# A graph-attention kernel: gathered rows side by side in one ring, one reduction over the places

## The chip, the cores and the metric

The kernel runs on one core of a Trainium2 chip. The metric is the device time of one execution in microseconds; the kernel before took 2087.87 us (median of three runs, 2083.0 to 2097.82). Besides these runs there is one execution under the hardware profiler, whose instructions are what "the trace" and "the page" mean below.

The engines are called as in the profile: PE (matrix multiply; PEld is its weight load), DVE (vector), ACT (scalar functions and copies), POOL (here mostly the issue of indirect transfers, the gathers and scatters) and SP (issue of plain transfers).

## The reference

A graph of N = 3327 nodes with 256 features each and a 0/1 adjacency matrix (each node has itself and on average 8 others as neighbours) goes through four layers: attention block, averaging layer, attention block, attention block. An attention block has 8 heads of 32:

```python
qkv = layer_norm(x, g1, be1) @ w_qkv
q, k, v = (qkv[:, 0], qkv[:, 1], qkv[:, 2])          # after reshape(n, 3, 8, 32)
scores = jnp.einsum('nhd,mhd->hnm', q, k) * SCALE
scores = jnp.where((adj != 0)[None], scores, -jnp.inf)
attn = jax.nn.softmax(scores, axis=-1)
out = jnp.einsum('hnm,mhd->nhd', attn, v).reshape(n, DIM)
x = x + out @ w_proj + b_proj
x = x + jax.nn.gelu(layer_norm(x, g2, be2) @ w1 + b1) @ w2 + b2
```

The averaging layer weighs a 64-wide projection of the neighbours' rows, projects it back, adds it to x and normalises.

## The kernel before

The kernel makes use of the sparsity: no 3327 x 3327 score matrix exists. A first stage (`adjacency`, 0 to 310 us) reads the matrix, makes for every node the list of its neighbours (at most 24), and sorts the nodes by the number of neighbours. The sorted nodes are cut into 26 tiles of 128 (one node per partition); `ROOM[t]` says how many neighbour places tile t needs, from 24 for tile 0 down to 4 for tile 25, 228 together. Beside this, `by_node` computes keys, values and queries of the first block into a table in DRAM.

Then come block 0 (310 to 760 us), the averaging layer (760 to 1064), block 1 (to 1605) and block 2 (to the end). A block goes through the tiles from the one with the fewest places to tile 0 with 24, in ten groups (`GROUPS`) of two to four tiles, the last two of one. For each tile:

- `scores` (L552): the tile's own row is fetched (keys, values, queries, features, 4 x 256 floats; L559 by an indirect transfer in block 0, L564 and L566 by plain ones in blocks 1 and 2). In blocks 0 and 1 ACT copies its features to `x[t]` (L568). ACT copies the query into a PSUM bank (L571, two banks in rotation). For each place an indirect transfer (`gather`, L546) fetches key and value (512 floats) of one neighbour per partition. Four places make one unit tile; ten units are in rotation (`UNITS`), and three own rows. For the own row and for each unit DVE multiplies the keys by the query (L576) and sums over each head's 32 (L577). Then follow the mask, the maximum, the subtraction and, on ACT, the exponential (L591 to L596).
- `weighed` (L599), called for the tile before, after the scores of the next: sum and reciprocal of the exponentials, the scaled weights (L605 to L607), the multiplication of all values by the weights (L610: own row, then each unit), and the additions: full units onto the first one (L622), the part unit (L626), halves of the unit onto each other (L630, 512 and 256 elements), and the last onto the own part (L631).
- After a whole group: transposes and projection (`project`), residual (L671), layer norm, the two feed-forward products (L685 and L695), and what the next stage needs (`finish`, `write`). Each product's bias comes by a small matmul of three bf16 parts (`bias`, L189) that opens the accumulation of each tile's 256 columns; two tiles share one PSUM bank.

The statements are recorded by a tile framework, which orders the instructions of each engine by its own planning and adds the waits: a gather into a unit waits until DVE has done with the unit's earlier content. Each engine works through its own order; what waits at the head holds what is behind it. The averaging layer borrows the same units for transposed parts of the adjacency matrix (L936) and for rows (L955).

Of the kernel before, what the change touches and what calls it, by code (L numbers as in the profile page):

```python
# [59 lines left out]
UNIT = 4  # L60
UNITS = 10
# [20 lines left out]
def chunk_width(c):  # L82
    return min(CW, NP - c * CW)


class Sparse:
# [100 lines left out]
    def bias(self, y, i):  # L187

        self.nc.tensor.matmul(y, self.ones3, self.biases[:, i, :], start=True, stop=False)  # L189
# [354 lines left out]

    def gather(self, out, table, t, j, held):
        g = self.nc.gpsimd.indirect_dma_start(  # L546
            out=out, out_offset=None, in_=table,
            in_offset=bass.IndirectOffsetOnAxis(ap=self.ids[:, t, j : j + 1], axis=0),
        )
        self.after(g, held)  # L550

    def scores(self, pool, pp, layer, t, held):  # L552


        nc = self.nc
        J = ROOM[t]
        own = pool.tile([P, 4 * DIM], F32, tag="own", name="own", bufs=3)
        if layer == 0:
# [14 lines left out]
        units = []  # L573

        def dot(at, k, n):
            nc.vector.tensor_mul(k, k, query.unsqueeze(1).to_broadcast([P, n, DIM]))  # L576
            nc.vector.tensor_reduce(  # L577
                s[:, ds(at, n), :].rearrange("p j h -> p (j h)"), k.rearrange("p j (h d) -> p j h d", d=HD), AX.X,
                ALU.add,
            )  # L580
# [10 lines left out]
        nc.vector.tensor_add(s[:, ds(1, J), :], s[:, ds(1, J), :], away)  # L591
        top = pool.tile([P, HEADS], F32, tag="top", name="top", bufs=3)
        nc.vector.tensor_reduce(top, s[:, : J + 1, :].rearrange("p j h -> p h j"), AX.X, ALU.max)
        wide = [P, J + 1, HEADS]
        nc.vector.tensor_sub(s[:, : J + 1, :], s[:, : J + 1, :], top.unsqueeze(1).to_broadcast(wide))
        nc.scalar.activation(s[:, : J + 1, :], s[:, : J + 1, :], AF.Exp)  # L596
        return own, s, units

    def weighed(self, pool, t, own, s, units):  # L599

        nc = self.nc
        J = ROOM[t]
        wide = [P, J + 1, HEADS]
        total = pool.tile([P, HEADS], F32, tag="total", name="total", bufs=3)
        nc.vector.tensor_reduce(total, s[:, : J + 1, :].rearrange("p j h -> p h j"), AX.X, ALU.add)  # L605
        nc.vector.reciprocal(total, total)
        nc.vector.tensor_mul(s[:, : J + 1, :], s[:, : J + 1, :], total.unsqueeze(1).to_broadcast(wide))  # L607

        def weigh(to, v, at, n):
            nc.vector.tensor_mul(  # L610
                to.rearrange("p j (h d) -> p j h d", d=HD), v.rearrange("p j (h d) -> p j h d", d=HD),
                s[:, ds(at, n), :].unsqueeze(3).to_broadcast([P, n, HEADS, HD]),
            )

        o = pool.tile([P, DIM], F32, tag="o", name="o", bufs=5)
        weigh(o.unsqueeze(1), own[:, DIM : 2 * DIM].unsqueeze(1), 0, 1)
        for u, j0, n in units:
            v = u[:, :n, DIM:]
            weigh(v, v, 1 + j0, n)
        full = [u for u, _, n in units if n == UNIT]  # L620
        for u in full[1:]:
            nc.vector.tensor_add(full[0][:, :, DIM:], full[0][:, :, DIM:], u[:, :, DIM:])  # L622
        u = full[0]
        for r, _, n in units:
            if n < UNIT:
                nc.vector.tensor_add(u[:, :n, DIM:], u[:, :n, DIM:], r[:, :n, DIM:])  # L626
        n = UNIT
        while n > 1:
            n //= 2
            nc.vector.tensor_add(u[:, :n, DIM:], u[:, :n, DIM:], u[:, ds(n, n), DIM:])  # L630
        nc.vector.tensor_add(o, o, u[:, 0, DIM:])  # L631
        return o

    def block(self, layer, weights, then, ahead=None, last=None):
# [4 lines left out]
        with tc.tile_pool(name="bs", bufs=1) as pool, tc.tile_pool(name="bp", bufs=1, space=PSUM) as pp:  # L639
            begin, finish, write = then(pool, pp) if then else (None, None, None)  # L640
            held = self.held

            def attended(t, own, s, units):
                o = self.weighed(pool, t, own, s, units)
                return t, o

            def halves(name, n):

                banks = [pp.tile([P, CW], F32, tag="mm", name=name, bufs=4) for _ in range(0, n, 2)]
                return [banks[q // 2][:, ds(q % 2 * DIM, DIM)] for q in range(n)]  # L650

            def project(group, outs):
# [8 lines left out]
                for q, y in enumerate(ys):  # L661
                    self.bias(y, 2 * layer)
                    for k in range(KC):
                        nc.tensor.matmul(y, oT[:, k, ts(q, P)], wpj[:, k, :], start=False, stop=k == KC - 1)  # L664
# [11 lines left out]
            def feed_forward(group, ys):  # L676
# [15 lines left out]
                for q, y in enumerate(ys):  # L692
                    self.bias(y, 2 * layer + 1)
# [887 lines left out]
```

## Time and profile before

| what | value |
|---|---|
| median of three runs | 2087.87 us (2083.0 to 2097.82) |
| the profiled execution | 2096.42 us, span of its instructions 2094.6 us |
| mean granted PE clock in it | 0.77 |
| instructions | 17222 |
| gathers (L546) | 684, 975 ns of POOL each |
| transfers | 369.73 MB, 169409 packets |
| features copied by ACT (L568) | 52 of 404 ns (median) |
| bias matmuls (L189) | 78 of 283 ns and 78 of 295 ns |

A line of the groups reads: source line, engine, operation, tile written <- tiles read, shapes (partitions x elements of a partition), count | busy time in us, mean ns of one | idle time of the engine just before these instructions, and what ended that idle time. A line of windows gives for a stretch of the span the busy time of each engine with its number of instructions.

### The profile page before, as it was taken

The numbers are of one execution on the slowest core, as the hardware profiler recorded it, in microseconds if no ns is written. First come the engines' busy times: TensorE is split into PE (matmuls) and PEld (weight loads), VectorE is DVE, ScalarE is ACT, GpSimd is POOL, SyncE is SP. The second block draws the span as 40 slices with busy tenths as digits, with TensorE's granted clock in tenths as the row PEclk, the third lists the DMA queues.
The fourth block names the chain that finished last, engine by engine and source line by source line (L and its number), as shares of the span: only waits on it lengthen the run. The fifth ranks groups of instructions, "written<-read, shape, count | busy, mean of one in ns | idle before, by whom it ended". The sixth has DMA issues, their size and how long they took to land. (4 is left out here: it accounts for less than half of the span.)

```text
span 2094.6 us, 17222 instructions
## 1 busy us (share of the span) xinstructions
PE 1263.4 (60%) x4806; PEld 812.1 (39%) x4806; DVE 1342.0 (64%) x3407; ACT 684.9 (33%) x1420; POOL 1001.0 (48%) x946
## 2 busy tenths in 40 slices
PE   3244411556755579699934688567695277655676
PEld 1122200344424337577512454343473154323445
DVE  3567635577776785165636789776732679976871
ACT  3555501233321224122322444334343133322232
POOL 3768757555555531101156645555203666565521
PEclk8667655677767769799976888798798587767778
DMA  8878827555555550858486656656215665565520
GB/s 191 330 300 326 284 79 213 160 163 154 170 148 175 147 131 23 198 154 230 160 284 205 216 166 209 220 178 193 61 56 201 210 186 176 176 190 160 152 65 20
DMA packets 169409, 369.73 MB, mean 177 GB/s; under 512 B 78821, under 2 KB 90291, under 8 KB 165976
## 3 DMA queue, kind: packets, MB, share of 16 engines
q0 software_dynamic: 68624, 222.01, 35.4%
q1 hardware_dynamic: 85689, 112.44, 17.1%
q10 hardware_dynamic: 14990, 34.08, 5.0%
q8 instruction: 40, 0.66, 0.1%
q14 instruction: 66, 0.54, 0.1%
HBM read 279.77 MB, written 77.59 MB: 171 GB/s over the span
## 5 line engine op out<-in xcount | busy, mean ns | idle before, releaser
L546 POOL DMA_INDIRECT unit<-kv,ids x684 | 667.2, 975 | 434.7 <-issue 189.1
L685 PE MATMUL f<-hT,w 128*128 128x256 f32 (+3 forms) x960 | 342.1, 517 | 58.6 <-ACT gT L688 23.2
L256 PE MATMUL tr<-ident,xh 128*128 128x128 f32 x312 | 80.6, 384 | 442.7 <-ACT xh L251 395.6
L695 PE MATMUL f<-w,gT 128*128 128x256 f32 x1248 | 306.4, 399 | 17.9 <-ACT gT L688 14.3
L685 PEld LDWEIGHTS f<-hT,w 128*128 128x128 f32 x960 | 190.4, 219 | 202.6 <-issue 106.0
L695 PEld LDWEIGHTS f<-w,gT 128*128 128x128 f32 x1248 | 238.3, 197 | 68.7 <-ACT gT L688 18.3
L256 PEld LDWEIGHTS tr<-ident,xh 128*128 128x128 f32 x312 | 41.7, 179 | 483.3 <-ACT xh L251 414.8
L576 DVE TENSOR_TENSOR unit<-unit,qs 128x1024 f32<-128x1024 f32 (+3 forms) x198 | 211.7, 1069 | 26.4 <-DMA unit<-kv,ids 15.0
L577 DVE TENSOR_REDUCE qs<-unit 128x32 f32<-128x1024 f32 (+3 forms) x198 | 212.7, 1074 | 4.8 <-DVE qs L607 1.7
L610 DVE TENSOR_TENSOR unit<-unit,qs 128x1024 f32<-128x1024 f32 (+3 forms) x198 | 210.0, 1065 | 0.0
L315 POOL TENSOR_TENSOR m<-a,place 128x3328 f16<-128x3328 fp8e4 x26 | 159.4, 6132 | 78.7 <-ACT a L313 78.6
L688 ACT ACTIVATE gT<-f,b 128x256 f32<-128x256 f32 (+3 forms) x240 | 124.8, 536 | 212.5 <-PE f L685 106.6
L538 PE MATMUL kvps<-wqkv,hT 128*128 128x512 f32 x312 | 171.9, 677 | 29.5 <-ACT hT L262 22.5
L326 DVE MAX8 found<-m 128x8 f16<-128x416 f16 x208 | 111.5, 579 | 39.7 <-POOL m L315 33.1
L664 PE MATMUL proj<-wproj,oT 128*128 128x256 f32 x312 | 109.3, 489 | 42.7 <-ACT oT L659 22.8
L576 DVE TENSOR_TENSOR own<-own,qs 128x256 f32<-128x256 f32 x78 | 32.3, 415 | 141.5 <-ACT qs L571 124.2
L658 PE MATMUL otr<-ident,o 128*128 128x128 f32 x156 | 25.5, 289 | 142.4 <-DVE qs L577 87.4
L990 POOL DMA_INDIRECT sorted<-st,to x26 | 24.8, 955 | 178.7 <-ACT st L542 147.1
L538 PEld LDWEIGHTS kvps<-wqkv,hT 128*128 128x128 f32 x312 | 63.2, 213 | 86.7 <-issue 37.7
L313 ACT ACTIVATE a<-a 128x3328 fp8e4<-128x3328 int32 x26 | 77.3, 2973 | 51.6 <-DMA kv<-st 29.0
L251 ACT ACTIVATE xh<-x,shift,rstd 128x256 f32<-128x256 f32 x104 | 58.4, 594 | 104.5 <-DVE shift L218 80.9
L664 PEld LDWEIGHTS proj<-wproj,oT 128*128 128x128 f32 x312 | 66.9, 235 | 65.6 <-ACT oT L659 28.4
(193 smaller groups left out, 1881.4 us busy)
## 6 DMA issues: line engine op xcount, KB each, us to landing
a<-in_adj SPq DMA_DIRECT2D x25, 1663.5 KB
kv<-st ACTq DMA_DIRECT2D x52, 512.0 KB
own<-sorted SPq DMA_DIRECT2D x26, 512.0 KB
unit<-kv,ids POOLq DMA_INDIRECT x684
adj<-a SPq DMA_DIRECT2D x26, 416.0 KB
own<-qkv SPq DMA_DIRECT2D x26, 384.0 KB
own<-own SPq DMA_DIRECT2D x26, 384.0 KB
w<-in_L_gnn_w SPq DMA_DIRECT2D x6, 1024.0 KB
```

What stands on the lines that cost most here:

```text
L256: nc.tensor.transpose(ps[k][:, ts(q, P)], t[:, ts(k, P)], self.ident)
L315: nc.gpsimd.tensor_mul(m.rearrange("p (s e) -> p s e", e=SEG), a8.rearrange("p (s e) -> p s e", e=SEG), place.unsqueeze(1).to_broadcast([P ...
L326: nc.vector.max(found[:, i, s, :], m[:, ts(s, SEG)])
L538: nc.tensor.matmul(kv, hT[:, k, ts(q, P)], w[:, k, DIM : 3 * DIM], start=k == 0, stop=k == KC - 1)
L546: g = self.nc.gpsimd.indirect_dma_start(out=out, out_offset=None, in_=table, in_offset=bass.IndirectOffsetOnAxis(ap=self.ids[:, t, j : j + ...
L576: nc.vector.tensor_mul(k, k, query.unsqueeze(1).to_broadcast([P, n, DIM]))
L577: nc.vector.tensor_reduce(s[:, ds(at, n), :].rearrange("p j h -> p (j h)"), k.rearrange("p j (h d) -> p j h d", d=HD), AX.X, ALU.add,)
L610: nc.vector.tensor_mul(to.rearrange("p j (h d) -> p j h d", d=HD), v.rearrange("p j (h d) -> p j h d", d=HD), s[:, ds(at, n), :].unsqueeze ...
L664: nc.tensor.matmul(y, oT[:, k, ts(q, P)], wpj[:, k, :], start=False, stop=k == KC - 1)
L685: nc.tensor.matmul(y[:, :w], w1[:, k, ts(f, P)], hT[:, k, :w], start=k == 0, stop=k == KC - 1)
L688: nc.scalar.activation(gT[-1][:, f % 2, :w], y[:, :w], AF.Gelu_apprx_tanh, bias=b1[:, f : f + 1])
L695: nc.tensor.matmul(y, gT[f // 2][:, f % 2, ts(q, P)], w2[:, f, :], start=False, stop=f == FC - 1)
```

## The change

All rows of a tile, gathered ones and its own, now lie side by side in one tile `ring` of 46 places of 512 floats (`RING`), in the order of the places with the own row (two places long) at the end. `take` hands out the places in rotation and begins again at the start when the rest is too short. Scores are computed in pieces of up to 6 places and weighed in pieces of up to 9, the own row among them, in pieces of nearly equal size. The weighed values are summed by one `tensor_reduce` over the places, whose input steps by a whole place from element to element, in place of the additions. The features go to `x[t]` by a transfer: in block 0 from the ring, in block 1 straight from DRAM; ACT's copy is gone. The bias matmul covers both 256-column halves of a bank at once, and only the last matmul of a bank closes its accumulation. The averaging layer takes four places at a time from the ring instead of a unit.

```diff
-UNIT = 4
-UNITS = 10
+RING = 46
+PIECE = 6
+WEIGHED = 9
...
+class Halves(list):
+    def __init__(self, banks, n):
+        super().__init__(banks[q // 2][:, ds(q % 2 * DIM, DIM)] for q in range(n))
+        self.banks = banks
+    def bank(self, q):
+        return self.banks[q // 2], min(2, len(self) - q)
+    def ends(self, q):
+        return q % 2 == 1 or q == len(self) - 1
...
-    def bias(self, y, i):
-        self.nc.tensor.matmul(y, self.ones3, self.biases[:, i, :], start=True, stop=False)
+    def bias(self, ys, q, i):
+        if q % 2 == 0:
+            bank, n = ys.bank(q)
+            self.nc.tensor.matmul(
+                bank[:, : n * DIM], self.ones3, self.biases[:, i, :].unsqueeze(1).to_broadcast([3, n, DIM]),
+                start=True, stop=False,
+            )
...
+    def take(self, n):
+        if self.at + n > RING:
+            self.at = 0
+        at = self.at
+        self.at += n
+        return self.ring[:, at : at + n, :]
...
-        own = pool.tile([P, 4 * DIM], F32, tag="own", name="own", bufs=3)
+        n = J + 1
+        rows = self.take(n + 1)
+        own = rows[:, J:, :].rearrange("p a b -> p (a b)")
         if layer == 0:
             nc.gpsimd.indirect_dma_start(
                 out=own, out_offset=None, in_=self.kv[0][:],
                 in_offset=bass.IndirectOffsetOnAxis(ap=self.row[t], axis=0),
             )
+            nc.sync.dma_start(out=self.x[t], in_=own[:, 3 * DIM :])
         elif layer == 1:
-            self.after(nc.sync.dma_start(out=own, in_=self.sorted[ts(t, P), :]), self.turning)
+            for to, at in ((own[:, : 3 * DIM], self.sorted[ts(t, P), : 3 * DIM]), (self.x[t], self.sorted[ts(t, P), 3 * DIM :])):
+                self.after(nc.sync.dma_start(out=to, in_=at), self.turning)
         else:
             nc.sync.dma_start(out=own[:, : 3 * DIM], in_=self.own[t])
-        if layer < 2:
-            nc.scalar.copy(self.x[t], own[:, 3 * DIM :])
+        for j in range(J):
+            self.gather(rows[:, j, :], self.places[layer], t, j, held)
...
-        dot(0, own[:, :DIM].unsqueeze(1), 1)
-        for j0 in range(0, J, UNIT):
-            n = min(UNIT, J - j0)
-            u = self.units.tile([P, UNIT, 2 * DIM], F32, tag="unit", name="unit")
-            for j in range(n):
-                self.gather(u[:, j, :], self.places[layer], t, j0 + j, held)
-            dot(1 + j0, u[:, :n, :DIM], n)
-            units.append((u, j0, n))
+        for lo, w in self.pieces(n, PIECE):
+            k = rows[:, ds(lo, w), :DIM]
+            nc.vector.tensor_mul(k, k, query.unsqueeze(1).to_broadcast([P, w, DIM]))
+            nc.vector.tensor_reduce(
+                s[:, ds(lo, w), :].rearrange("p j h -> p (j h)"), k.rearrange("p j (h d) -> p j h d", d=HD), AX.X,
                 ALU.add,
             )
...
+    def pieces(n, most):
+        count = -(-n // most)
+        at = 0
+        for k in range(count):
+            w = (n - at) // (count - k)
+            yield at, w
+            at += w
...
+        for lo, w in self.pieces(n, WEIGHED):
+            v = rows[:, ds(lo, w), DIM:].rearrange("p j (h d) -> p j h d", d=HD)
+            nc.vector.tensor_mul(v, v, s[:, ds(lo, w), :].unsqueeze(3).to_broadcast([P, w, HEADS, HD]))
         o = pool.tile([P, DIM], F32, tag="o", name="o", bufs=5)
-        weigh(o.unsqueeze(1), own[:, DIM : 2 * DIM].unsqueeze(1), 0, 1)
-        for u, j0, n in units:
-            v = u[:, :n, DIM:]
-            weigh(v, v, 1 + j0, n)
-        full = [u for u, _, n in units if n == UNIT]
-        for u in full[1:]:
-            nc.vector.tensor_add(full[0][:, :, DIM:], full[0][:, :, DIM:], u[:, :, DIM:])
-        u = full[0]
-        for r, _, n in units:
-            if n < UNIT:
-                nc.vector.tensor_add(u[:, :n, DIM:], u[:, :n, DIM:], r[:, :n, DIM:])
-        n = UNIT
-        while n > 1:
-            n //= 2
-            nc.vector.tensor_add(u[:, :n, DIM:], u[:, :n, DIM:], u[:, ds(n, n), DIM:])
-        nc.vector.tensor_add(o, o, u[:, 0, DIM:])
+        nc.vector.tensor_reduce(o, rows[:, :n, DIM:].rearrange("p j f -> p f j"), AX.X, ALU.add)
         return o
...
-                    at = self.units.tile([P, NT // 2, HALF], BF, tag="unit", name="at")
+                    at = self.take(4).rearrange("p a b -> p (a b)").bitcast(BF)[:, : NT // 2 * HALF]
...
-                        both = self.units.tile([P, 2, 4 * DIM], F32, tag="unit", name="st4")
+                        both = self.take(4).rearrange("p (n a) b -> p n (a b)", n=2)
...
-        with tc.tile_pool(name="units", bufs=UNITS) as self.units:
+        with tc.tile_pool(name="gathered", bufs=1) as pool:
+            self.ring, self.at = pool.tile([P, RING, 2 * DIM], F32, name="ring"), 0
```

More of the change, by code (lines that the diff above doesn't have):

```diff
@@ L572, in scores @@
         s = bank[:, ds(DIM, (SLOTS + 1) * HEADS)].rearrange("p (j h) -> p j h", h=HEADS)
-        units = []
-        def dot(at, k, n):
-            nc.vector.tensor_mul(k, k, query.unsqueeze(1).to_broadcast([P, n, DIM]))
+        for lo, w in self.pieces(n, PIECE):
+            k = rows[:, ds(lo, w), :DIM]
+            nc.vector.tensor_mul(k, k, query.unsqueeze(1).to_broadcast([P, w, DIM]))
             nc.vector.tensor_reduce(
-                s[:, ds(at, n), :].rearrange("p j h -> p (j h)"), k.rearrange("p j (h d) -> p j h d", d=HD), AX.X,
+                s[:, ds(lo, w), :].rearrange("p j h -> p (j h)"), k.rearrange("p j (h d) -> p j h d", d=HD), AX.X,
@@ L579, in dot @@
                 ALU.add,
             )
[L582 to L589 removed]
         away = self.away[:, t, :J].unsqueeze(2).to_broadcast([P, J, HEADS])
[L591 removed]
+        nc.vector.tensor_add(s[:, :J, :], s[:, :J, :], away)
@@ L592, in scores @@
         top = pool.tile([P, HEADS], F32, tag="top", name="top", bufs=3)
[L593 to L599, printed above, removed]
+        nc.vector.tensor_reduce(top, s[:, :n, :].rearrange("p j h -> p h j"), AX.X, ALU.max)
@@ L601, in weighed @@
+        nc.vector.tensor_sub(s[:, :n, :], s[:, :n, :], top.unsqueeze(1).to_broadcast([P, n, HEADS]))
+        nc.scalar.activation(s[:, :n, :], s[:, :n, :], AF.Exp)
+        return rows, s
+    @staticmethod
+    def pieces(n, most):
[5 more added lines that the diff above has]
+            at += w
+    def weighed(self, pool, t, rows, s):
         nc = self.nc
-        J = ROOM[t]
-        wide = [P, J + 1, HEADS]
+        n = ROOM[t] + 1
@@ L604, in weighed @@
         total = pool.tile([P, HEADS], F32, tag="total", name="total", bufs=3)
-        nc.vector.tensor_reduce(total, s[:, : J + 1, :].rearrange("p j h -> p h j"), AX.X, ALU.add)
+        nc.vector.tensor_reduce(total, s[:, :n, :].rearrange("p j h -> p h j"), AX.X, ALU.add)
         nc.vector.reciprocal(total, total)
[L607 to L613, printed above, removed]
@@ L627, in weighed @@
-        n = UNIT
-        while n > 1:
-            n //= 2
-            nc.vector.tensor_add(u[:, :n, DIM:], u[:, :n, DIM:], u[:, ds(n, n), DIM:])
-        nc.vector.tensor_add(o, o, u[:, 0, DIM:])
+        nc.vector.tensor_mul(s[:, :n, :], s[:, :n, :], total.unsqueeze(1).to_broadcast([P, n, HEADS]))
+        for lo, w in self.pieces(n, WEIGHED):
+            v = rows[:, ds(lo, w), DIM:].rearrange("p j (h d) -> p j h d", d=HD)
+            nc.vector.tensor_mul(v, v, s[:, ds(lo, w), :].unsqueeze(3).to_broadcast([P, w, HEADS, HD]))
@@ L641, in block, with attended @@
             held = self.held
-            def attended(t, own, s, units):
-                o = self.weighed(pool, t, own, s, units)
-                return t, o
+            self.at = 0
+            def attended(t, rows, s):
+                return t, self.weighed(pool, t, rows, s)
             def halves(name, n):
-                banks = [pp.tile([P, CW], F32, tag="mm", name=name, bufs=4) for _ in range(0, n, 2)]
-                return [banks[q // 2][:, ds(q % 2 * DIM, DIM)] for q in range(n)]
+                return Halves([pp.tile([P, CW], F32, tag="mm", name=name, bufs=4) for _ in range(0, n, 2)], n)
             def project(group, outs):
@@ L661, in project @@
                 for q, y in enumerate(ys):
-                    self.bias(y, 2 * layer)
+                    self.bias(ys, q, 2 * layer)
                     for k in range(KC):
-                        nc.tensor.matmul(y, oT[:, k, ts(q, P)], wpj[:, k, :], start=False, stop=k == KC - 1)
+                        nc.tensor.matmul(
+                            y, oT[:, k, ts(q, P)], wpj[:, k, :], start=False, stop=k == KC - 1 and ys.ends(q)
+                        )
                 return ys
@@ L692, in feed_forward @@
                 for q, y in enumerate(ys):
-                    self.bias(y, 2 * layer + 1)
+                    self.bias(ys, q, 2 * layer + 1)
                     for f in range(FC):
                         nc.tensor.matmul(
-                            y, gT[f // 2][:, f % 2, ts(q, P)], w2[:, f, :], start=False, stop=f == FC - 1
+                            y, gT[f // 2][:, f % 2, ts(q, P)], w2[:, f, :], start=False, stop=f == FC - 1 and ys.ends(q)
                         )
@@ L935, in sums @@
                 for lo in range(0, n // 2):
-                    at = self.units.tile([P, NT // 2, HALF], BF, tag="unit", name="at")
+                    at = self.take(4).rearrange("p a b -> p (a b)").bitcast(BF)[:, : NT // 2 * HALF]
+                    at = at.rearrange("p (g i) -> p g i", i=HALF)
                     nc.sync.dma_start_transpose(
```

## The prediction

> **What bounds the kernel now.** I read the page's busy times first, then stage windows, then groups by form, and last the waits and the chain.
>
> ```profile
> PE 1263.4 (60%) x4806; PEld 812.1 (39%) x4806; DVE 1342.0 (64%) x3407; ACT 684.9 (33%) x1420; POOL 1001.0 (48%) x946
> ```
>
> No engine is full, so the stages decide. The windows below (start and end, length, busy of PE, PEld, DVE, ACT, POOL, granted clock, DMA share, GB/s) are the adjacency stage, block 0, the averaging, block 1 and block 2.
>
> ```profile
> 0.00:310.00 310.00, 107.00 (x303) 55.55 (x303) 169.63 (x583) 128.99 (x157) 202.65 (x131) 0.69 0.76 252
> 310.00:760.00 450.00, 235.86 (x810) 153.47 (x810) 316.77 (x698) 123.40 (x302) 259.22 (x267) 0.70 0.57 167
> 760.00:1064.00 304.00, 269.82 (x1441) 189.27 (x1442) 154.91 (x550) 92.48 (x208) 37.01 (x40) 0.91 0.56 155
> 1064.00:1605.00 541.00, 367.94 (x1257) 229.69 (x1256) 356.52 (x834) 207.76 (x472) 250.83 (x255) 0.81 0.55 176
> 1605.00:2095.00 490.00, 282.81 (x995) 184.11 (x995) 344.14 (x744) 132.24 (x282) 251.28 (x255) 0.75 0.50 152
> ```
>
> The change is in the blocks, 1481 us; DVE is the busiest engine in blocks 0 and 2, and in block 1 PE is level with it. Block 2 cut finer shows two regimes:
>
> ```profile
> 1605.00:1700.00 95.00, 30.69 (x97) 21.19 (x97) 55.14 (x135) 17.46 (x44) 58.83 (x61) 0.60 0.65 202
> 1700.00:1800.00 100.00, 58.03 (x209) 39.72 (x210) 89.37 (x204) 31.84 (x68) 62.09 (x63) 0.76 0.61 190
> 1800.00:1900.00 100.00, 69.32 (x195) 37.91 (x195) 74.89 (x155) 32.07 (x56) 57.38 (x60) 0.75 0.57 169
> 1900.00:2000.00 100.00, 59.01 (x213) 38.67 (x213) 76.76 (x143) 20.23 (x41) 60.78 (x61) 0.78 0.57 166
> ```
>
> In the chain that ended last, 1609 to 1731 us is almost all gathers, one per 1.25 us (0.95 and a gap of 0.30): POOL binds there and DVE is 58% busy at first. From 1734 on the chain is mostly DVE with stretches of PE and a few gathers, and POOL in turn waits for DVE to give back buffers:
>
> ```profile
> L546 POOL DMA_INDIRECT unit<-kv,ids x684 | 667.2, 975 | 434.7 <-issue 189.1 <-DVE o L631 64.4 <-DVE unit L622 54.7
> L576 DVE TENSOR_TENSOR own<-own,qs 128x256 f32<-128x256 f32 x78 | 32.3, 415 | 141.5 <-ACT qs L571 124.2 <-DMA own<-own 12.0 <-issue 5.4
> ```
>
> The second line is the other half of that loop: DVE waits 124 us for the query copy, and that copy (L571) waits 78 us for the last weighing of an earlier tile. So DVE's length per tile matters in the later tiles and much less in the first twelve.
>
> **The sum over places.** The groups of before, by form:
>
> ```profile
> L577 DVE TENSOR_REDUCE qs<-unit 128x32 f32<-128x1024 f32 x144 | 175.7, 1220 | 2.2 <-remote 1.6 <-DVE qs L607 0.5
> L622 DVE TENSOR_TENSOR unit<-unit 128x1024 f32<-128x1024 f32 x66 | 80.2, 1216 | 0.0
> L630 DVE TENSOR_TENSOR unit<-unit 128x256 f32<-128x256 f32 x78 | 32.5, 417 | 1.8 <-DVE qs L591 1.2 <-DVE qs L595 0.5
> ```
>
> 1216 ns for 1024 elements and 417 for 256 give 1.04 ns an element. In the timeline, back to back, a 1024-element operation follows its predecessor after 1.13 us, though it is listed with 1.21; so an instruction occupies DVE for elements x 1.04 ns + 0.065 us. The neighbour lists sum to J = 228 places a block, 254 with the own ones.
>
> Before, the additions (L622, L626, L630, L631) are 354 instructions over 3 x 228 x 256 = 175,104 elements: 182 + 23 = 205 us. After, 78 reductions run over 3 x 254 x 256 = 195,072 elements. Their inner step is one place, 512 floats, so each element is read 2 KB from the one before. The trace has one sizeable reduction that jumps in SBUF (L382 reads `p t l -> p l t`, a step of 25 floats) and one of nearly the same shape without jumps:
>
> ```profile
> L382 DVE TENSOR_REDUCE larger<-more 128x25 bf16<-128x650 f32 x1 | 1.3, 1317 | 0.0
> ...
> L442 DVE TENSOR_REDUCE count<-tops 128x26 f32<-128x624 f32 x1 | 0.8, 793 | 0.0
> ```
>
> Taking 0.15 us off each as the fixed part of a duration, that is 1.80 against 1.03 ns an element. L382 also writes bf16, but L377 turns 650 fp32 elements into bf16 in 823 ns, the ordinary rate, so I lay the difference on the jumps. Bounds for the new sum: 195,072 x 1.04 ns + 78 x 0.065 = 208 us from below (the row without jumps), 195,072 x 2.03 ns (L382 with no fixed part) + 5 = 401 us from above. I take 1.80, the row that jumps: 351 + 5 = 356 us. Change: +151 (+3 to +196).
>
> The Trainium skill speaks for the lower end: "VectorE: DVE Perf Modes", section "Mode 1× (REGULAR) — the baseline", says that this mode, the only one a reduction has, gives one result a cycle and takes weird strides too. By it the sum would be the 208 us; the trace's L382 contradicts it. "Advanced Engine Details and Errata", section "SBUF Cachelines", says the other thing, that accesses to ever new 16-byte lines pay a penalty, without a size.
>
> **Larger pieces.** Scores (L576, L577) and weighing (L610) keep their elements: 508 + 254 places a block. Their instructions fall from 552 + 276 to 324 + 117 in all, 387 x 0.065 = -25 us. The same skill page, section "The TRN2 errata", puts the measured fixed part of a DVE operation near 150 cycles; by that, the 663 instructions gone with the additions' would be worth some 104 us (estimate) and not 43. The timeline's 1.13 us starts show that most of a duration's fixed part overlaps the neighbour.
>
> DVE in all: +151 - 25 = **+126 us** (-22 to +171), 42 a block. A tile of J places changes by (J+1) x 0.195 - 0.28 us: +0.7 at J=4, +1.5 at J=8, +4.6 at J=24.
>
> **How much is on the path.** The first twelve tiles (J sums to 72) carry 84 x 0.195 - 12 x 0.28 = 13 us of the 42; POOL's gathers hide them, and it would be +13 a block without that cover. The other 14 tiles carry 29 us. There the release of a tile's places lets the gathers run, which let the scores run, so the added time goes round the loop; but DVE has some 40 us of idle in 1731 to 2000, part of it waits for PE (L671) that a later DVE finds already over. I count 4 us as swallowed and 25 as paid, three blocks: +75. Bounds: 0, and all 42 x 3 = 126.
>
> **The ring.** Ten units of 4 places and three own rows of 2 make 46 places, as does the ring. Held against each other tile by tile, the ring's wrap cuts the last tiles short: the own row (its query gates every score) of J=12 and J=24 tiles goes where the tile two before lay, and waits for that tile's whole sum; before, it waited for the weighing three tiles back. In the trace such an own load that came late cost DVE 12.0 us once (row L576 above). Three or four such tiles a block: 0 from below, 12 us a block from above, taken as 0, since the scheduler can put another tile's weighing in between. All places of a tile now come back at once, after the sum; before, 4-place units came back one by one (POOL's L622 waits). This is in the loop above.
>
> **Features by a transfer.** 52 ACT copies of 404 ns (L568) go, 21 us of ACT, which is 33% busy; their waits for the own row (86.5 and 36.8 us) pass to the query copy, which needs the same row. SP issues 52 more transfers at 0.32 us; in block 0 each waits on SP for its own gather, and nothing that is soon needed stands behind it (begin's weights are ahead; the averaging's first transposes, at 765 us, come after the last of them and need free places anyway). In block 1 all features load at the stage's start. Gathers that reuse an own row now also wait for that transfer. Worth 0 to -21; taken as 0, as ACT's copies lie beside DVE's work. Uncovered it would be the query 0.4 us earlier.
>
> **One bias matmul for two halves.** 156 of some 280 ns become 90 of twice the columns: at most -18 us of PE at 60%, at least 0 (twice the columns at twice the time, +6). Only the last groups' PE chain (2030 to 2080) has no cover: taken as 0.
>
> **Sum.** The profiled execution took 2096.4 us (span 2094.6), 8.5 above the median of 2087.9. 2096.4 + 75 = 2171, and in terms of the median **2163 us**, +3.6%.
>
> **Rivals.**
> - *The jump costs nothing* (faster). If DVE reads a 2 KB step at 1.04 ns, DVE loses 22 us; two thirds count (29 of 42): -15; the copies and the bias matmuls may give another -15: 2058. It decides at the price where DVE's sum is level: (205 + 25 - 5) / 195,072 = 1.15 ns an element, 2.95 us for ten places. For it: L908, a strided 26-element read, takes 178 ns, as its unstrided neighbours do (26 elements are few). Against it: L382.
> - *The jump costs, but the idle of DVE swallows it*: DVE idles 464 us in the blocks, so +126 fits. At most a quarter is paid: 2088 + 0 to 31, say 2100. Against: POOL's waits for DVE (o, unit) show that the idle is itself part of the loop.
> - *The ring binds on top*: the own row late by 12 us a block, and all 42 paid from the first tile: 2088 + 126 + 36 = 2250, its lower half from 2205.
>
> **Chances.** Forecast 0.54 (2115 to 2205), jump free 0.20 (2035 to 2075), swallowed 0.13 (2080 to 2120), ring 0.13 (2205 to 2260). A measurement of this kernel can tell about 1% from no change: faster means below 2067, slower above 2109. Faster 0.16 (most of the free jump), same 0.11 (its rest and half of swallowed), slower 0.73. The range 2060 to 2235 leaves out about 0.11 below and 0.05 above; the forecast's own is 2115 to 2205.
>
> **What would show it.** Right: a reduction `o<-ring` with 128x2560 elements at about 4.7 us (ten places) and some 356 us in all; DVE near 1465 busy; the blocks 20 to 30 us longer each, the averaging within 5 us; the first 120 us of block 2 still at one gather per 1.25 us; L622 to L631 and the L568 copies gone. Wrong: that reduction at 2.8 us (free jump); DVE up with spans unchanged (swallowed); long waits of the query copy for own loads, or of POOL for a transfer, in the J=12 to J=24 tiles (ring).

## The result, and the profile after

The changed kernel takes **2161.17 us** (median of four runs, 2149.99 to 2164.51) against 2092.51 us for the kernel before in the same comparison (four runs, 2083.0 to 2097.82): 1.0324 times as long, 95% interval 1.0266 to 1.0381. The forecast was 2163 us, slower. The total fits; the parts that make it up do not, and the experiments are about that.

The first line of the changed kernel's page, the busy times:

```profile
PE 1244.6 (58%) x4740; PEld 817.9 (38%) x4740; DVE 1453.1 (67%) x2744; ACT 671.3 (31%) x1370; POOL 977.0 (45%) x946
```

DVE has 111.1 us more to do (1342.0 before) with 663 instructions fewer; PE, ACT and POOL have a little less. (The expectations below call DVE, PE, ACT, POOL and SP VectorE, TensorE, ScalarE, GpSimd and SyncE.) The windows of the changed kernel are cut here by its own indirect transfers, which give sharp marks: the adjacency stage, block 0 up to its last scatter into `between`, the averaging up to block 1's first gather, block 1 up to block 2's first gather, and block 2. The columns are those of the windows before.

```profile
0.00:311.00 311.00, 106.71 (x303) 55.13 (x303) 172.26 (x590) 130.81 (x177) 200.05 (x129) 0.69 0.75 249
311.00:837.00 526.00, 296.16 (x1129) 205.13 (x1129) 399.37 (x604) 152.02 (x356) 264.72 (x280) 0.74 0.59 169
837.00:1088.00 251.00, 203.89 (x1101) 139.19 (x1101) 106.85 (x414) 57.66 (x110) 28.36 (x32) 0.87 0.55 159
1088.00:1663.00 575.00, 364.01 (x1234) 233.65 (x1234) 392.41 (x613) 197.07 (x445) 241.22 (x254) 0.78 0.53 167
1663.00:2160.00 497.00, 273.80 (x973) 184.79 (x973) 382.18 (x523) 133.72 (x282) 242.70 (x254) 0.74 0.49 143
```

Cut at the same marks, the trace of before has 847.5 us to the end of block 0, then 223.7, 537.8 and 485.6. (The stages given ahead of the result end block 0 at 760 us. Its scatters into `between` run on to 847.6 us, so block 0 was 88 us longer and the averaging 80 us shorter than was taken there.) So the 65 us between the two spans are made up as follows: block 0 ends 10.8 us *earlier*, the averaging is **27.5 us longer**, block 1 is 37.4 longer, block 2 11.0 longer. DVE's additional work is spread evenly over the blocks (35 to 38 us each); the time is not.

The groups of the changed kernel by form, the new sum and beside it a product over adjacent words:

```profile
L609 DVE TENSOR_TENSOR ring<-ring,qs 128x1280 f32<-128x1280 f32 x75 | 110.8, 1481 | 70.0 <-DMA ring<-kv,ids 63.2 <-ACT qs L605 3.5 <-issue 2.0
...
L644 DVE TENSOR_REDUCE o<-ring 128x256 f32<-128x2560 f32 x12 | 54.2, 4520 | 0.4 <-PE otr L670 0.4
...
L644 DVE TENSOR_REDUCE o<-ring 128x256 f32<-128x6400 f32 x3 | 33.3, 11101 | 0.1
...
L644 DVE TENSOR_REDUCE o<-ring 128x256 f32<-128x1280 f32 x6 | 13.9, 2312 | 0.0
```

From 1280 to 6400 elements the sum grows by 8.79 us, 1.72 ns an element; the product of the first line does 1280 elements in 1.48 us where the sum takes 2.31. All 78 sums take 343.5 us.

In the averaging the difference stands in one group. PE's groups of that stage, first of before, then of after:

```profile
L944 PE MATMUL ups<-at,parts 128*128 128x256 fp8e4 (+1 forms) x676 | 78.2, 275 | 0.0
```

```profile
L959 PE MATMUL ups<-ring,parts 128*128 128x256 fp8e4 (+1 forms) x676 | 86.3, 291 | 16.5 <-DMA ring<-adj 16.5
```

The sums over neighbours, which never waited, now wait 16.5 us for the transposed adjacency; and the same products take 8.1 us more, with a granted clock of the stage of 0.87 instead of 0.92. PE is busy for 204 of the 251 us, so both count.

### The profile page after: what moved, and what is told of

It is laid out like the page before. It is cut to its first block, busy times and chain, and to the rows that moved or that the text cites. A ratio compares the mean times of both kernels' runs of the same rounds, so it can differ in the third digit from the quotient of the medians.

```text
span 2159.7 us, 16455 instructions
## 1 busy us (share of the span) xinstructions
PE 1244.6 (58%) x4740; PEld 817.9 (38%) x4740; DVE 1453.1 (67%) x2744; ACT 671.3 (31%) x1370; POOL 977.0 (45%) x946
## 5 line engine op out<-in xcount | busy, mean ns | idle before, releaser
L575 POOL DMA_INDIRECT ring<-kv,ids x684 | 647.4, 947 | 454.4 <-issue 191.7
L644 DVE TENSOR_REDUCE o<-ring 128x256 f32<-128x1792 f32 (+9 forms) x78 | 343.5, 4404 | 1.3 <-issue 0.8
L709 PE MATMUL f<-w,gT 128*128 128x256 f32 x1248 | 297.8, 394 | 39.9 <-issue 33.9
L609 DVE TENSOR_TENSOR ring<-ring,qs 128x1280 f32<-128x1280 f32 (+3 forms) x162 | 226.6, 1403 | 92.7 <-DMA ring<-kv,ids 64.7
L709 PEld LDWEIGHTS f<-w,gT 128*128 128x128 f32 x1248 | 240.0, 196 | 93.2 <-issue 53.6
L610 DVE TENSOR_REDUCE qs<-ring 128x40 f32<-128x1280 f32 (+3 forms) x162 | 227.3, 1408 | 15.1 <-remote 6.6
L642 DVE TENSOR_TENSOR ring<-ring,qs 128x1280 f32<-128x1280 f32 (+4 forms) x117 | 219.2, 1883 | 2.5 <-DVE qs L615 1.2
L685 DVE SCALAR_TENSOR_TENSOR x<-f,x 128x256 f32<-128x256 f32 x78 | 30.5, 417 | 134.1 <-PE f L709 83.4
L1005 POOL DMA_INDIRECT sorted<-ring,to x26 | 25.0, 963 | 206.1 <-ACT ring L563 167.9
L676 PE MATMUL proj<-wproj,oT 128*128 128x256 f32 x312 | 95.4, 455 | 28.6 <-ACT oT L671 26.9
L670 PE MATMUL otr<-ident,o 128*128 128x128 f32 x156 | 26.8, 305 | 145.5 <-issue 103.9
L605 ACT COPY qs<-ring 128x256 f32<-128x256 f32 x78 | 29.2, 376 | 217.0 <-DVE ring L642 89.6
```

Source lines behind the costliest of these rows:

```text
L575: g = self.nc.gpsimd.indirect_dma_start(out=out, out_offset=None, in_=table, in_offset=bass.IndirectOffsetOnAxis(ap=self.ids[:, t, j : j + ...
L610: nc.vector.tensor_reduce(s[:, ds(lo, w), :].rearrange("p j h -> p (j h)"), k.rearrange("p j (h d) -> p j h d", d=HD), AX.X, ALU.add,)
L642: nc.vector.tensor_mul(v, v, s[:, ds(lo, w), :].unsqueeze(3).to_broadcast([P, w, HEADS, HD]))
L644: nc.vector.tensor_reduce(o, rows[:, :n, DIM:].rearrange("p j f -> p f j"), AX.X, ALU.add)
L709: nc.tensor.matmul(y, gT[f // 2][:, f % 2, ts(q, P)], w2[:, f, :], start=False, stop=f == FC - 1 and ys.ends(q))
```

## The experiments

All edited kernels load the adjacency in the averaging by plain transfers: the transposition is left out, the sums there are of other nodes, and everything else is as it was. A transposing load was not run in an edited kernel. So the study has its own two base kernels, `c0_before` and `e0_changed`. The runs went to several chips, and the kernel before takes a different time on them: 1908 us on one, some 2070 to 2090 us on the others ("quick" and "slow" below). Kernels are compared on one kind of chip only.

All profiled runs cut at the marks used above, in us:

| run | chip | to the end of block 0 | averaging | block 1 | block 2 | span |
|---|---|---|---|---|---|---|
| before | slow | 847.5 | 223.7 | 537.8 | 485.6 | 2094.6 |
| after | slow | 836.8 | 251.2 | 575.2 | 496.6 | 2159.7 |
| c0_before | quick | 788.6 | 225.6 | 476.3 | 420.6 | 1911.2 |
| e0_changed | quick | 757.1 | 228.4 | 499.7 | 439.1 | 1924.3 |
| e1_adjacent_b | quick | 747.6 | 228.4 | 482.8 | 407.0 | 1865.9 |
| e2_halves_b | quick | 764.2 | 228.0 | 459.1 | 411.0 | 1862.4 |
| f0_before | slow | 837.4 | 224.5 | 526.8 | 482.0 | 2070.7 |
| f1_changed | slow | 841.6 | 234.7 | 567.9 | 496.8 | 2141.0 |
| f2_apart | slow | 839.2 | 231.8 | 570.8 | 489.6 | 2131.4 |
| e4_copies_b | slow | 841.0 | 230.8 | 569.2 | 489.6 | 2130.6 |
| e0_again | slow | 833.7 | 228.9 | 563.3 | 487.5 | 2113.4 |
| e2_again | slow | 813.0 | 228.5 | 536.9 | 474.7 | 2053.1 |
| e5_pieces | slow | 842.4 | 228.9 | 538.8 | 507.1 | 2117.1 |
| e6_ring40 | slow | 865.2 | 246.9 | 565.4 | 513.4 | 2190.9 |

### The two base kernels: plain loads

```diff
-                    nc.sync.dma_start_transpose(
-                        out=at, in_=self.adj[ds(c * P + lo * HALF, HALF), :].bitcast(BF)
-                    )
+                    nc.sync.dma_start(
+                        out=at.rearrange("p g i -> p (g i)"),
+                        in_=self.adj[ds(c * P + lo * HALF, HALF), :].bitcast(BF).rearrange("(p n) f -> p (n f)", n=2),
+                    )
```

In the kernel before:

> The kernel before, whose 13 transposing loads of the adjacency in the averaging are plain loads of the same bytes: the transposition is left out, and the sums over neighbours are of other nodes. All further kernels of this study have this edit too, so that they are compared with this one and with the changed kernel so edited. If the blocks don't feel it, as both theories hold, block 0 and the blocks 1 and 2 stand within 1% of 847.6, 537.8 and 485.6 us, and only the averaging (223.6 us) can move.

In the changed kernel:

> The changed kernel with the plain loads of the adjacency and nothing else. Theory (a load of the adjacency into the one ring waits there for rows that nodes some chunks before still hold): the averaging stays 15 to 30 us longer than that of the kernel before with the same edit, and TensorE's sums over neighbours wait for the load again; the blocks are longer by the 37 us of the first comparison. Rival (the transposing loads themselves were slow in the changed kernel): the averaging falls to within 8 us of the kernel before so edited, and the whole distance of 69 us to about 45.

`c0_before`: 1910.52 us, 1.0001 of the kernel before on that chip (0.998 to 1.0022). The edit costs the kernel before nothing. The expected stage times were missed by 7 to 13%, all in the blocks: they were taken from a slow chip.

`e0_changed`: 1925.57 us, 1.0073 of the kernel before (1.005 to 1.0096). With plain loads the averaging is 228.4 us against 225.6: the excess of 27.5 us is gone, as the *rival* expected (on a slow chip too: 228.9 us in `e0_again`). The whole distance is 17.5 us and not about 45: on the quick chip the blocks differ by -31.5, +23.4 and +18.5 us.

### The sum over adjacent words

```diff
-        nc.vector.tensor_reduce(o, rows[:, :n, DIM:].rearrange("p j f -> p f j"), AX.X, ALU.add)
+        flat = rows.rearrange("p j f -> p (j f)")[:, : n * DIM]
+        nc.vector.tensor_reduce(o, flat.rearrange("p (f j) -> p f j", j=n), AX.X, ALU.add)
```

> The changed kernel with plain loads of the adjacency, whose sum over the places reads as many numbers, but adjacent ones (the first n x 256 of the tile's rows) instead of one word in every 2 KB; it no longer sums the values of the places, all else stands. Theory (the jump of 2 KB is what the sum costs, and VectorE's time counts in the blocks): the 78 sums take 195,072 x 1.043 ns + 78 x 0.15 us = 215 us instead of 343.5, and of these 128 us less the blocks give back between a third (the blocks grew by 38 us for 111 us more of VectorE) and six tenths (the forecast's 75 of 126): 44 to 77 us below the changed kernel with plain loads; the averaging stays. Rival, the sum lies in VectorE's idle time: 215 us as well, but less than 12 us are given back. Rival, the access is not what costs: the sums stay above 300 us.

Measured: 1869.8 us, **55.8 us less than `e0_changed`**; 0.9787 of the kernel before (0.9759 to 0.9815). The groups by form of this kernel, the same three sizes as above:

```profile
L645 DVE TENSOR_REDUCE o<-ring 128x256 f32<-128x2560 f32 x12 | 33.8, 2813 | 0.1
...
L645 DVE TENSOR_REDUCE o<-ring 128x256 f32<-128x6400 f32 x3 | 20.4, 6811 | 0.0
...
L645 DVE TENSOR_REDUCE o<-ring 128x256 f32<-128x1280 f32 x6 | 8.9, 1483 | 0.0
```

1.04 ns an element; 214.6 us in all, where 215 was expected. Number of elements, of sums and of results are the same, so the step of 2 KB is what costs, 0.68 ns an element. DVE's busy time falls by 125.8 us (1446.5 to 1320.7), and the kernel gets back 44% of that. Idle time swallows the larger part, but not all: the rival of the swallowed sum (less than 12 us) falls.

### The sum by halves in place

```diff
-        nc.vector.tensor_reduce(o, rows[:, :n, DIM:].rearrange("p j f -> p f j"), AX.X, ALU.add)
+        while n > 1:
+            h = n // 2
+            to = o.unsqueeze(1) if n == 2 else rows[:, :h, DIM:]
+            nc.vector.tensor_add(to, rows[:, :h, DIM:], rows[:, ds(n - h, h), DIM:])
+            n -= h
```

> The changed kernel with plain loads of the adjacency, whose sum over the places is made by additions by halves in place: the first h places plus the last h, until one is left; 282 additions over adjacent words instead of 78 sums with jumps. Theory: 175,104 numbers x 1.04 ns + 282 x 0.15 us = 224 us instead of 343.5, and the blocks give back a third to six tenths of these 119 us: 40 to 71 us below the changed kernel with plain loads. Rival, the number of instructions is what counts and not the jump: 204 instructions more cost 13 us at 0.065 us each, 0 to 14 us above it. Rival, the sum lies in idle time: within 10 us of it.

Measured on the quick chip: 1866.91 us, 58.7 below `e0_changed`, and **0.9769 of the kernel before** (0.9743 to 0.9794). Two lines of its groups, and between them how DVE's idle time moved; first `e0_changed`:

```profile
L644 DVE TENSOR_REDUCE o<-ring 128x256 f32<-128x1792 f32 (+9 forms) x78 | 343.6, 4405 | 0.5 <-PE otr L670 0.4
...
L609 DVE TENSOR_TENSOR ring<-ring,qs 128x1280 f32<-128x1280 f32 (+3 forms) x162 | 226.5, 1403 | 73.6 <-DMA ring<-kv,ids 65.2 <-ACT qs L605 7.4
```

Then this kernel:

```profile
L609 DVE TENSOR_TENSOR ring<-ring,qs 128x1280 f32<-128x1280 f32 (+3 forms) x162 | 227.1, 1403 | 132.2 <-DMA ring<-kv,ids 73.6 <-ACT qs L605 48.0 <-issue 9.1
...
L647 DVE TENSOR_TENSOR ring<-ring 128x768 f32<-128x768 f32 (+6 forms) x204 | 192.5, 943 | 0.2
...
L647 DVE TENSOR_TENSOR o<-ring 128x256 f32<-128x256 f32 x78 | 32.5, 418 | 0.5 <-PE otr L674 0.4
```

The sum falls from 343.6 to 225.0 us (224 expected), with 204 instructions more. DVE is busy 134.8 us less. Of this the kernel gets 58.7; the idle ahead of the key products (L609) rises by 58.6, of which 40.6 is the wait for the query copy: DVE now reaches a tile before its query is there.

On a slow chip, beside the base kernel on the same chip:

> The changed kernel with plain loads of the adjacency again, beside the next three kernels. The chips of this study stand apart: on one the kernel before takes some 1908 us, and this kernel took 1.007 times that; on the others 2080 to 2092 us, and there the changed kernel as it is took 1.032 times that, with an averaging 27 us longer, which plain loads shorten by some 20. So 1.007 on the quick chip, 1.020 to 1.026 on a slow one.

> The changed kernel with plain loads and the sum by halves again. On the quick chip VectorE had 119 us less to do than with the jumping sum, and the kernel took 59 us less (0.50 of it). Theory (the same share on a slow chip, as the jump is VectorE's and not the chip's): 40 to 75 us below the changed kernel with plain loads, and below the kernel before. Rival (on a slow chip the engines idle 120 us more with nothing that they wait for, and 282 instructions in place of 78 bring more of that): less than 30 us below it, and not below the kernel before.

`e0_again`: 2117.52 us, 1.027 of the kernel before (1.0164 to 1.0376), just above what was expected. `e2_again`: 2056.78 us, **60.7 us less**, with 136.8 us less of DVE: the same share, 44%. Against the kernel before it is 0.9962 (0.9908 to 1.0016), which is not told from no change. So the jumping sum costs some 60 us on both kinds of chip, and all else that the change does in the blocks and the averaging (with plain loads) gives back 41 us on the quick chip (1908.0 - 1866.9) and some 8 on the slow one (0.9962 of the kernel before; the interval includes zero).

Both edits do one thing more. The sum over adjacent words reads only the first half of a tile's rows, and the first addition of the halves is done with the last ones, so rows come back to the ring before the sum is complete. In `e0_changed` POOL's gathers wait 65.4 us for a finished sum (`o` L644: 49.8 at L575 and 15.6 at L591). In `e1_adjacent_b` they wait 26.1 us for the weighing ahead of the sum (L642) and not for the sum itself. How much of the 56 to 61 us is this earlier return, and how much the shorter sum, is not separated.

Where a block pays also shows. On the quick chip the first twelve tiles' gathers take the same time with either sum (the 72nd goes out after 104.2, 89.5 and 93.2 us in the three blocks of `e0_changed`, after 103.9, 88.9 and 93.1 in `e1_adjacent_b`). From there to the last gather `e1_adjacent_b` is 65 us shorter. These fourteen tiles have 170 of the 254 places, some 86 of the 129 us of the sums' difference (estimate). On the slow chip `e2_again` is ahead of `e0_again` by 5 to 10 us a block at the 72nd gather already.

How the 60 us fall on the blocks differs from run to run: block 0 gets 7 us longer by the halves on the quick chip and 20.7 shorter on the slow one. A single block's difference of 20 us can't be read as an effect of one edit.

### The ring in the averaging

Three kernels, with loads in pieces of 256 bytes in place of the transposing ones; the third with the ring divided:

```diff
+                    for m in range(2):
+                        nc.sync.dma_start(
+                            out=at[:, :, ts(m, P)],
+                            in_=self.adj[ds(c * P + lo * HALF + m * P, P), :].bitcast(BF).rearrange("p (g k) -> p g k", k=P),
+                        )
```

```diff
-                    at = self.take(4).rearrange("p a b -> p (a b)").bitcast(BF)[:, : NT // 2 * HALF]
+                    slot = (c // 4 * 2 + lo) % 4 * 4
+                    at = self.ring[:, ds(slot, 4), :].rearrange("p a b -> p (a b)").bitcast(BF)[:, : NT // 2 * HALF]
...
-                        both = self.take(4).rearrange("p (n a) b -> p n (a b)", n=2)
+                        slot = 16 + t // 2 % 7 * 4
+                        both = self.ring[:, ds(slot, 4), :].rearrange("p (n a) b -> p n (a b)", n=2)
```

> The kernel before, whose transposing loads of the adjacency are loads in pieces of 256 bytes (3,328 packets a load, as the transposing loads had some 3,344 of under 512 bytes; untransposed, so the sums are of other nodes). The averaging stays within 8 us of 225 us if ten units that come free in any order cover a slow load.

> The changed kernel with the same loads in pieces of 256 bytes. With plain, quick loads its averaging was as short as the one before (228.4 and 225.6 us), with transposing loads 27 us longer. Theory (a load starts late, when the ring's turn comes to rows that nodes still hold, and a slow load then lands too late): TensorE waits for the load again, the averaging is 10 to 30 us longer than that of the kernel before with these loads. Rival (the transposing loads were held up by something of their own, as the packets in flight beside them, not by the ring's order): within 8 us of it.

> The changed kernel with loads in pieces of 256 bytes, and the ring divided in the averaging: the adjacency takes turns in the first 16 rows, the nodes' rows in the next 28. Theory (the ring's order makes the loads late): the averaging returns to within 8 us of the kernel before with these loads, and TensorE does not wait for the adjacency. Rival: as long as the undivided ring's.

Averaging: 224.5, 234.7 and 231.8 us; whole kernels 2072.45, 2143.13 and 2133.24 us (one run each). PE's waits in the averaging of `f1_changed` (us in total, times, longest):

```profile
PE ups L961 <- DMA ring<-adj: 5.5, 3, 2.8
```

In `f2_apart` PE's longest wait for the adjacency is gone; that line's own view has

```profile
  DMA ring<-adj: 0.2, 1
```

and the time from the first to the last scatter into `sorted` goes from 152.5 to 147.2 us (146.1 in `f0_before`). The kernel before with these loads does not wait. So the theory's wait is there, at a third of the size: with these loads the ring's order makes PE wait 5.5 us, with the transposing ones it was 16.5, with quick ones nothing. But dividing the ring wins only 2.9 of the 10.2 us of excess. Of the 7.3 us that remain, 6 lie ahead of the first scatter (77.6 against 71.5 us from block 0's last one); what makes them was not found.

The trace of the changed kernel itself shows which loads are late. PE's three waits end at 930.5, 965.1 and 1001.8 us, and SP issues three loads 12 to 15 us before, at 915.8, 953.0 and 987.4 us. The last pair, from the timelines:

```profile
987.37 6.47 SPq L952 DMA_TRANSPOSE ring<-adj  x1
```

```profile
1001.76 2.50 PE L959 MATMUL ups<-ring,parts 128*128 128x256 fp8e4 x11 [6.43 <-DMA ring<-adj]
```

In the trace of before no load is issued less than 21.8 us ahead of the products that read it, counting both in order, and PE waits for none.

The kernel with a shorter ring, told below, says the same from the other side: with plain, quick loads and 40 rows, that is ten turns of four instead of eleven, PE waits again and the averaging is 18.0 us longer than `e0_again`'s. Its waits of PE and of SP's queue there:

```profile
PE ups L960 <- DMA ring<-adj: 16.4, 4, 5.7
```

```profile
SPq L952 <- DMA sorted<-ring,to: 126.5, 6, 51.6
```

A load of the adjacency stands on SP's queue until the `sorted` scatter of an earlier chunk has left the rows that are next in turn. Such a wait by itself does not make PE wait: SP's queue has 64.9 us of them in the kernel before, whose loads still go out early enough. The kernel before has ten units as well, and there PE did not wait at all. Its units don't go round in strict turn: in its program the loads of the fourth chunk take the two units that those of the second left, ahead of the units of nodes that were taken sooner. So ten turns of room are enough when units are handed out as they come free, and not in this fixed order with these loads. That the transposing loads' excess comes from this alone was not tried: no run divides the ring under them.

### Features by ACT's copies again

```diff
-            nc.sync.dma_start(out=self.x[t], in_=own[:, 3 * DIM :])
...
-            for to, at in ((own[:, : 3 * DIM], self.sorted[ts(t, P), : 3 * DIM]), (self.x[t], self.sorted[ts(t, P), 3 * DIM :])):
-                self.after(nc.sync.dma_start(out=to, in_=at), self.turning)
+            self.after(nc.sync.dma_start(out=own, in_=self.sorted[ts(t, P), :]), self.turning)
...
+        if layer < 2:
+            nc.scalar.copy(self.x[t], own[:, 3 * DIM :])
```

> The changed kernel with plain loads of the adjacency, with the features copied by ScalarE from the own row again (blocks 0 and 1), the own row of block 1 loaded whole. 52 copies of some 0.4 us return to ScalarE, 52 transfers of 128 KB leave SyncE's queue. Forecast's step (the transfers are worth nothing): within 6 us of 1925. Theory of the part that gives back (block 0 became 31 us shorter by the change although VectorE has 37 us more to do there, and only there do the transfers replace copies that wait on ScalarE for the own row, 117.7 us ahead of other work): block 0 longer by 10 to 30 us, block 2 the same. Rival (the transfers cost, as block 1, with two loads for one, became longer): block 1 shorter by 8 us or more.

Measured: 2131.24 us, 1.0239 of the kernel before (1.0167 to 1.0311), beside 1.027 for the changed kernel with plain loads on another slow chip (the 1925 us of the expectation are of the quick one). The copies are there again (ACT busy 687.1 us against 672.3), and no stage is more than 8 us from that of `e0_again`, less than single blocks differ from run to run. The transfers are worth nothing that can be measured across these two chips; an effect of the 10 to 30 us that the theory gave to block 0 is not seen (7.3 us).

### Smaller pieces

```diff
-PIECE = 6
-WEIGHED = 9
+PIECE = 2
+WEIGHED = 2
```

> The changed kernel with plain loads, with scores and weighing in pieces of at most 2 places instead of 6 and 9: 765 instructions of VectorE more over the same numbers. Forecast's price (0.065 us an instruction, between back-to-back starts): 50 us of VectorE's time, of which the blocks pay about half, 20 to 35 us above the changed kernel with plain loads. Rival (the fixed part of a duration, 0.15 us, or more where instructions come late): 115 us, 50 to 90 us above it. Rival (larger pieces are worth nothing, as they wait for more places to land): within 8 us of it, or faster.

Measured: 2122.78 us, 5.3 above `e0_again`; 1.0308 of the kernel before (1.0231 to 1.0386). The page's busy line of `e0_again`, then of `e5_pieces`:

```profile
PE 1242.8 (59%) x4740; PEld 818.3 (39%) x4740; DVE 1452.5 (69%) x2744; ACT 672.3 (32%) x1370; POOL 979.4 (46%) x946
```

```profile
PE 1229.0 (58%) x4740; PEld 808.0 (38%) x4740; DVE 1502.1 (71%) x3509; ACT 693.3 (33%) x1386; POOL 977.4 (46%) x946
```

765 instructions more cost DVE 49.6 us: 0.065 us each, exactly the forecast's price. By listed durations the three groups grew by 108.6 us (673.4 to 782.0), 0.142 each; most of an instruction's fixed part lies beside its neighbour. The Trainium skill's page "VectorE: DVE Perf Modes", section "The TRN2 errata", puts the fixed part near 150 cycles, some 0.157 us by the forecast's 104 us for 663 instructions; the listed durations come near that, the time that an instruction occupies DVE does not.

But the kernel pays only 5.3 us for those 49.6, inside both intervals: the rival "larger pieces are worth nothing" holds. The trace shows one thing on the other side: DVE's waits for gathered rows ahead of L609 fall from 63.5 to 30.7 us, as one would expect where a small piece waits for two places and not for six. All idle time ahead of L609 falls less, from 87.7 to 80.7 us.

### A shorter ring

```diff
-RING = 46
+RING = 40
```

> The changed kernel with plain loads and a ring of 40 rows instead of 46. Theory (the ring is no bound, the gathers come early enough): within 10 us of the changed kernel with plain loads. Rival (the ring binds, and own rows and gathers wait for rows that a sum before still reads): six rows less cost 10 to 30 us in each block, 30 to 90 us in all, and GpSimd's waits for the sum grow by as much.

With 40 rows the last two tiles of a block (16 and 26 rows) don't fit side by side: the last one's rows overwrite those of the one before ahead of its weighing, so that this tile sums other values, and waits for the last tile's gathers. Measured: 2193.32 us, 75.8 above `e0_again`; 1.0643 of the kernel before (1.0564 to 1.0723). 18.0 of it is the averaging. In the blocks the cost comes late. Counted from a block's first gather, the 177th (in the 23rd of 26 tiles) goes out after 322.1 us in block 1 (`e0_again` 322.8) and 300.0 in block 2 (306.1); the 181st, in the 24th tile, after 344.9 (327.8) and 329.8 us (311.1). To the 23rd tile six rows less cost nothing, and from there 17 to 19 us, before the overwritten tile comes into play. So the theory holds for the small tiles and the rival from the 24th tile on: there the ring is a bound. Block 1 ends only 2.1 us later all the same, block 0 31.5 and block 2 25.9; how much of these two is the overwritten tile's additional wait is not separated.

## Why the prediction was right in total and wrong in its parts

- **The price of the jump: right, a little high.** 1.72 ns an element against 1.80; 343.5 us against 356. `e1_adjacent_b` shows that it is the step. DVE in all +111 us against +126.
- **What of it is paid: the step "How much is on the path" failed.** It let 25 of 42 us a block count, six tenths, because little beside the first twelve tiles' share was to be covered (25 of the other fourteen's 29 us paid). `e1_adjacent_b`, `e2_halves_b` and `e2_again` give 0.44 of DVE's time three times over. On the quick chip the first twelve tiles are covered as forecast, and the other fourteen give back 65 of some 86 us in `e1_adjacent_b`, so more is swallowed there than was taken; the idle of DVE from 1731 to 2000 us, put at some 40 us, is 54 (269 less 215.3 busy). The jumping sum costs 56 to 61 us, the later return of the rows included, and not 90 (0.6 of 151).
- **"25 per block" failed in each block.** Measured -10.8, +37.4 and +11.0, in sum 37.6 instead of 75: the jumping sum's 60, less what else the change brings in the blocks. That rest was booked at -15 (six tenths of the -25 for larger pieces). It is 41 us on the quick chip; on the slow ones it is some 22 us here (60 less 37.6), some 8 in `e2_again`, and nothing between `f0_before` and `f1_changed`, whose blocks differ by 60 us.
- **Larger pieces: right for DVE, wrong as a gain.** 0.065 us an instruction held; on the kernel's time it is worth 5 us for twice that number of instructions.
- **"The averaging within 5 us" failed.** The forecast looked at the ring only tile by tile in the blocks. The averaging takes turns in the same ring. Three of the adjacency's loads go out there only 12 to 15 us before PE has them, where the kernel before leaves 22 us or more, and PE, busy for four fifths of that stage, waits for them for 16.5 of the 27.5 us. That the strict order of turns delays them is shown for loads of 256-byte pieces (5.5 us of waiting, 0.2 with the ring divided) and argued for the transposing ones. The blocks fell short of the forecast by 37.4 us and the averaging added 27.5 that it did not have: that these nearly cancel, and 2163 came so close, is luck.
- **Features: right** as far as two chips can be compared, 0 (`e4_copies_b`). **Bias matmul**: not tried by itself.
- **The rivals.** "The jump costs nothing" falls, but what it would have brought is seen: with a sum over adjacent words the same kernel is 2.1 to 2.3% faster than the kernel before on the quick chip, and with the sum by halves level on a slow one. "Swallowed" falls as a whole, though 56% is swallowed. "The ring binds on top": the waits it named are there, as POOL's own-row gathers in block 0 show in the waits of the changed kernel,

```profile
POOL ring L591 <- DVE o L644: 41.2, 3, 20.5
```

  but block 0 is shorter than before all the same, in this comparison (4.2 us longer in `f1_changed` than in `f0_before`). `e6_ring40` shows that the ring is short of binding harder by less than six rows, in the tiles with 12 to 24 places, as the step "The ring" had it.
- **Still open:** what gives back the 41 us on the quick chip, and whether anything is given back on a slow one. `e2_halves_b` has 26.0 us less of DVE than `c0_before`, with 459 instructions fewer; at 0.44 that is 11 us. The features' transfers and the size of the pieces, tried on slow chips, show no gain of that size. What remains is the own row's share in common instructions, the finer allotment of rows in the ring, and the bias matmuls; none of these was tried alone.

## What to carry to other kernels

A reduction over an outer index is one instruction, but here its elements lay 2 KB apart and cost 1.72 ns each instead of 1.04; additions by halves over whole rows did the same sum in two thirds of DVE's time, in spite of 204 more instructions. When a buffer that several stages borrow changes from units handed out as they come free to one ring in strict order, look at the order of turns in each stage that borrows it, and first in the one whose bounding engine had no wait. And a total that comes out as predicted says little until it is cut by stage.

## What the runs showed of the hardware

- **The step.** The Trainium skill's "VectorE: DVE Perf Modes", section "Mode 1× (REGULAR) — the baseline", says that weird strides work in this mode, and gives it one result a cycle. The same reduction with the same shapes took 4520 ns with a step of 2 KB and 2813 ns over adjacent words (128x2560). The measurement decides.
- **Chips differ by 8 to 10%.** The kernel before took 1908.03 us on one chip and some 2070 to 2090 us on the others (each chip was used in one stretch of time only, so the chip and the time are not told apart). DVE's busy time is nearly the same (1337.7 us in `c0_before` on the quick chip, 1342.9 in `f0_before` on a slow one; PE 1229.4 and 1262.8), and the 33rd gather of block 1 goes out 40.1 us after the first on both. What differs most is idle time for which the trace has no releaser on this core. DVE's waits of `f0_before`, two of many such lines:

```profile
DVE x L671 <- remote: 29.4, 4, 10.6
...
DVE total L605 <- issue: 20.4, 7, 9.4
```

  In all, such lines come to 72.5 us ("issue") and 47.4 us ("remote") of DVE, against 0.4 us in `c0_before`. What stands behind it was not found. The change costs more where this happens: 1.027 against 1.0073 with the same edit, so a ratio measured on one chip is not that of another.
